# Changing the walk of a column-phase add in a four-direction scan kernel

## The chip, the cores and the metric

The kernel runs on one core of one Trainium2 chip. The metric is the device time of one execution in microseconds (us); the time of a kernel is the median of its runs. The engines are named as in the profile: PE is TensorE (matmuls; PEld is its weight load), DVE is VectorE, ACT is ScalarE, POOL is GpSimd, and SP issues transfers. SBUF is the on-chip buffer of 128 partitions, PSUM the buffer that matmuls write into.

## The reference

The input x has 4 batches, 128 channels and 96 x 96 pixels, in fp32. It is normalized in groups of 4 channels, and then goes through the same gated scan four times: along the rows forwards and backwards, and along the columns forwards and backwards.

```python
seq_all = concat([rows, rows reversed, columns, columns reversed])
t = grouped1x1(seq, in_proj_w, in_proj_b, 4);  u, gate = t[:, :256], t[:, 256:]
u = depthwise_conv(silu(u), dw_w, 5 taps)
s = ssm_in_w u;  a = 0.999 + 0.0009 * sigmoid(ssm_delta_w u + b);  a = clip(a, 0.0001, 0.9999)
bb = tanh(ssm_b_w u + b);  cc = tanh(ssm_c_w u + b)
prefix = cumsum(log(a));  h = exp(prefix) * cumsum(bb * s * exp(-prefix))
u = u + ssm_out_w (cc * h + ssm_d * s)
y = out_proj_w (grouped1x1(u * sigmoid(gate), mix_w, mix_b, 4)) + out_proj_b
out = x + fuse_w concat(y of the four directions, each put back in pixel order) + fuse_b
```

The sum over the four directions is what the changed instruction takes part in.

## The kernel before

The channels lie on the partitions, and the 96 x 96 pixels of one batch along the free dimension. Three large buffers stay in SBUF: `xn` (the normalized input), `sil` (its silu projection) and `acc`, the accumulator of the output, stored row by row as [128, 96 rows, 96 columns]. `acc` starts as x.

For each batch there are two phases. V walks the columns; the host supplies x with its two spatial axes swapped (`xv`), so `xn` and `sil` lie in column order in that phase. H walks the rows. A phase has two passes, one per direction: V goes forwards in pass 0 and backwards in pass 1, H the other way round. A pass goes through 20 chunks of whole lines, 18 of five lines (480 pixels) and 2 of three (288 pixels, the last two in pixel order). With 4 batches these are 16 passes and 320 chunks, 160 of them in V.

The order of the work is the order in which the program is written: each engine executes its instructions in that order, and the tile framework adds the waits. One turn of the main loop (L386 and on) does the following.

- `conv_and_gate` of the chunk: five conv taps for channels 0 to 127 as matmuls with diagonal weights (L249), five taps for channels 128 to 255 as one ScalarE scaling (L260) and four DVE multiply-adds (L262), and the gate (matmul L271, sigmoid L275).
- `ssm_out` of the chunk before: two matmuls (L325, L329) and three DVE operations (L330 to L332).
- In pass 1, `front` of a chunk of the next phase: its normalization (L213), projection (L225) and silu (L229, L232), after a load of its x into `xn`.
- In pass 0 of V, the statistics of the next batch (L134), except for the last batch.
- `scan` of the chunk: projections (L288), three activations (L293, L295, L299), two GpSimd operations on the decay (L301, L302), the product b * s (L303), the recurrence (L309), whose state goes on to the next chunk, and c * h + d * s (L318, L319).
- `accumulate` of the chunk before: two matmuls with the fused output weights into the PSUM tile `py` (L340), and the add into `acc`. In V it is L345; in H it is L351 in pass 0 and L354 in pass 1, which also adds the bias and writes `res`, from where the result goes to memory.

`py` has a single PSUM buffer, so the next chunk's output matmuls wait until the add has read it. In V the chunk is in column order: `py` holds column after column of 96 pixels each, without a gap. The add reads and writes `acc` through the view `accT`, with its two axes swapped, so that it walks the same columns:

```python
accT = acc.rearrange("p h w -> p w h")
part = accT[:, bass.ds(STARTS[c], LINES[c]), :]
nc.vector.tensor_add(part, py[:, :n].rearrange("p (w h) -> p w h", h=HH), part)
```

A column's neighbouring pixels lie 96 words apart in `acc`. In H all operands of the add are contiguous.

Of the kernel before, what the change touches and what calls it, by code (L numbers as in the profile page):

```python
"""x + fuse(four-direction gated SSM scan of groupnorm(x)), one core, fp32 throughout.

For each batch there are two phases, one per pixel order: V walks the columns (its input is
x with the two spatial axes swapped, laid out so by the host) and H walks the rows. In a
phase silu(in_proj(groupnorm(x))) lies whole in SBUF, and both directions of that order read
it, one pass each. A pass goes through chunks of whole lines in scan order and carries the
state h from chunk to chunk:

    u   = depthwise conv of silu       (channels 0..127 on TensorE, 128..255 on ScalarE/VectorE)
    s, b, c, a = projections of u  # L10
    h   = a * h + b * s                (the recurrence behind exp(P) * cumsum(b*s*exp(-P)))
    v   = (u + ssm_out (c*h + d*s)) * sigmoid(gate)
    acc += W v                         (W = fuse_dir . out_proj . mix, multiplied out on chip)

A reverse direction uses flipped taps and scans its chunk backwards, so it stays in the pixel
order of its phase. acc starts as x (the residual). While the second pass of a phase runs, the
next phase's input is loaded into the chunks that are done with, and its silu computed.
"""
# [1 line left out]

# [10 lines left out]
P = 128  # L31
B, DIM, HH, WW = 4, 128, 96, 96
# [6 lines left out]
LINES = [5] * 18 + [3] * 2  # L39
STARTS = [sum(LINES[:i]) for i in range(len(LINES))]  # L40
# [5 lines left out]
def conv_preact_kernel(  # L46
# [27 lines left out]
    xn = big.tile([P, L], F32, name="xn")  # L74
    acc = big.tile([P, HH, WW], F32, name="acc")
    sil = big.tile([P, 2, L + 2 * PAD], F32, name="sil")
    accf = acc.rearrange("p h w -> p (h w)")
    accT = acc.rearrange("p h w -> p w h")

    srcs = {"V": xv, "H": xh}  # L80
    # (pixel order, [(reverse, index of the direction in fuse_w) of both passes])
    kinds = [("V", [(False, 2), (True, 3)]), ("H", [(True, 1), (False, 0)])]
    phases = [(b, order, passes) for b in range(B) for order, passes in kinds]

    def span(c):
        return bass.ds(STARTS[c] * WW, LINES[c] * WW)

# [1 line left out]
    gmean = wp.tile([P, P], F32, name="gmean")  # L89
    per = DIM // GN_GROUPS  # L90
    nc.gpsimd.memset(gmean, 1.0 / per)
    for base, step, mult in ((0, -per, 1), (per - 1, per, -1)):
        nc.gpsimd.affine_select(
            out=gmean,
# [38 lines left out]
        nc.sync.dma_start(t[:, :n], xh[b, :, span(c)])  # L133
        nc.vector.bn_stats(stats_of(b)[:, c, :], t[:, :n])  # L134

# [1 line left out]
    b0, order0, _ = phases[0]  # L137
    for c in range(NCH):
        nc.sync.dma_start(xn[:, span(c)], srcs[order0][b0, :, span(c)])
# [64 lines left out]
            )  # L204
        nc.vector.tensor_add(b_fin, pb[:, 0:1], b_fuse)

# [1 line left out]
    def front(ph, c):  # L208
        """groupnorm and silu(in_proj) of one chunk of phase ph, whose x lies in xn."""
        b = phases[ph][0]  # L210
        n = LINES[c] * WW
        norm = stats[b]
        nc.vector.tensor_scalar(  # L213
            xn[:, span(c)],
            xn[:, span(c)],
            norm[:, 0:1],
            norm[:, 1:2],
            ALU.subtract,
            ALU.mult,
        )  # L220
        pts = []
        for j in range(2):
            q = slice(32 * j, 32 * j + 32)
            pt = ps.tile([P, 512], F32, tag="ps_x", bufs=2, name=f"pu_{ph}_{c}_{j}")
            nc.tensor.matmul(pt[:, :n], w_in[q, :], xn[q, span(c)], start=True, stop=True)  # L225
            pts.append(pt)
        for j in range(2):
            sg = wk.tile([P, CW], F32, tag="sg", name=f"sg_{ph}_{c}_{j}")
            nc.scalar.activation(  # L229
                sg[:, :n], pts[j][:, :n], AF.Sigmoid, bias=b_in[:, j : j + 1]  # L230
            )
            nc.vector.scalar_tensor_tensor(  # L232
                sil[:, j, bass.ds(PAD + STARTS[c] * WW, n)],
                pts[j][:, :n],
                b_in[:, j : j + 1],
                sg[:, :n],
                ALU.add,
                ALU.mult,
            )
# [94 lines left out]
    def accumulate(st):  # L334
        c, d, gv = st["c"], st["dir"], st["gv"]
        n, id_ = LINES[c] * WW, st["id"]
        b, order, _ = phases[st["ph"]]
        py = ps.tile([P, 512], F32, tag="ps_y", name=f"py_{id_}")
        for j in range(2):
            nc.tensor.matmul(  # L340
                py[:, :n], w_fin[:, d, j, :], gv[:, j, :n], start=(j == 0), stop=(j == 1)
            )
        if order == "V":
            part = accT[:, bass.ds(STARTS[c], LINES[c]), :]
            nc.vector.tensor_add(  # L345
                part, py[:, :n].rearrange("p (w h) -> p w h", h=HH), part
            )
            return
        part = accf[:, span(c)]
        if st["pass"] == 0:  # L350
            nc.vector.tensor_add(part, py[:, :n], part)  # L351
            return
        res = wk.tile([P, CW], F32, tag="res", name=f"res_{id_}")
        nc.vector.scalar_tensor_tensor(  # L354
            res[:, :n], py[:, :n], b_fin, part, ALU.add, ALU.add
        )
        nc.sync.dma_start(out[b, :, span(c)], res[:, :n])
        if b + 1 < B:
            nc.sync.dma_start(part, xh[b + 1, :, span(c)])

# [1 line left out]
    steps = []  # L362
    for ph, (b, order, passes) in enumerate(phases):
        for ip, (rev, d) in enumerate(passes):
# [16 lines left out]
    for c in range(NCH):  # L381
        front(0, c)
# [3 lines left out]
    for n, st in enumerate(steps):  # L386
        b, order, _ = phases[st["ph"]]
        conv_and_gate(st)
        if st["pass"] == 1 and st["ph"] + 1 < len(phases):
            nb, norder, _ = phases[st["ph"] + 1]  # L390
            nc.sync.dma_start(xn[:, span(st["c"])], srcs[norder][nb, :, span(st["c"])])
            todo.append((n + 2, st["ph"] + 1, st["c"]))
        if prev is not None:
            ssm_out(prev)
        while todo and todo[0][0] <= n:
            _, ph, c = todo.pop(0)
            front(ph, c)
        if order == "V" and st["pass"] == 0 and b + 1 < B:
            stats_chunk(b + 1, st["c"])
            if st["i"] == NCH - 1:  # L400
                stats_finish(b + 1)
        scan(st)
        if prev is not None:
            accumulate(prev)
        prev = st
    ssm_out(prev)
    accumulate(prev)


# [54 lines left out]
```

## Time and profile before

| what | value |
| --- | --- |
| time, two runs | 3685.1 and 3701.43 us |
| median | 3693.26 us |
| the profiled execution: span from its first to its last instruction | 3681.5 us |
| mean granted TensorE clock in it | 0.938 |
| adds of the V phases, L345 | 160 instructions, 163.9 us busy |
| adds of the H phases, L351 and L354 | 160 instructions, 105.1 us busy |
| loads and stores | 25 GB/s on average over the span |

The profile gives a span for the profiled execution and no separate time; the lowest of the two runs is 3.6 us above that span and the median 11.8 us. The page has the busy time of each engine, the groups of instructions by line (count, busy time, mean duration of one, and the idle time of the engine just before them with what ended it), and the chain of work that ended last, followed back from the last instruction. A stretch of the span can be asked for alone; its row has the length of the stretch, the busy time of each engine with its number of instructions, the granted TensorE clock (1.00 is full speed), the share of the DMA engines and the GB/s that they moved.

### The profile page before, as it was taken

The page shows a single profiled execution, that of the slowest core. Times are in us where ns is not written, and L with a number is a line of the kernel's source. Part 1 is how long each engine was busy: PE and PEld are TensorE (multiplying, and loading weights), DVE is VectorE, ACT ScalarE, POOL GpSimd, SP SyncE. Part 2 cuts the span into 40 slices and gives each one's busy share as a digit, 9 for nine tenths or more (in the row PEclk, how much of TensorE's full clock was granted, in tenths as well). Part 3 has the DMA queues.
Part 4 walks back from the last instruction along what each step waited for, and adds up shares of the span by engine and source line. Part 5 has one row for each costly group of instructions (what it writes and reads, how often), then busy time and mean ns, then how long its engine had stood idle before and what let it go on. Part 6 is the DMA issues. An engine that isn't in the chain of part 4 may idle for free.

```text
span 3681.5 us, 27637 instructions
## 1 busy us (share of the span) xinstructions
PE 3543.3 (96%) x9032; PEld 1550.5 (42%) x9032; DVE 2937.6 (80%) x4442; ACT 1572.0 (43%) x2572; POOL 393.2 (11%) x653
## 2 busy tenths in 40 slices
PE   7999999999999999999999999999999999999999
PEld 3334444444443444444443444444444344444444
DVE  7788887788877888778887788777887778877777
ACT  3334444444443444444443444444444444444443
POOL 0011111111111111111111011111111111111111
PEclk8899999999999999999999999999999999999999
DMA  4210000002100000001210000000121000000000
GB/s 145 82 37 12 19 22 0 0 30 65 59 3 0 17 19 17 0 0 46 65 45 0 0 20 22 11 0 3 59 62 32 0 4 21 22 6 0 3 24 25
DMA packets 56625, 92.14 MB, mean 25 GB/s; under 512 B 7296, under 2 KB 56352, under 8 KB 56480
## 3 DMA queue, kind: packets, MB, share of 16 engines
q1 hardware_dynamic: 54720, 89.68, 8.0%
q8 instruction: 70, 1.15, 0.1%
q10 hardware_dynamic: 1760, 0.70, 0.1%
q14 instruction: 75, 0.61, 0.1%
HBM read 71.48 MB, written 18.87 MB: 25 GB/s over the span
## 4 chain that ended last, share of the span: by engine, by line
DVE 46%; PE 41%; issue 6%; ACT 4%; DMA 2%; POOL 0%; ACTq 0%; DVEq 0%; POOLq 0%
DVE u L262 12%; PE pp L288 8%; PE pc L325 8%; PE pc L249 8%; DVE h L309 8%; PE py L340 6%; PE pz L329 6%; DVE z L319 5%; DVE tb L303 4%; DVE z L318 4%; DVE gv L332 3%; PE pu L225 3%; DVE u L331 3%; DVE sil L232 3%; ACT u L260 2%
## 5 line engine op out<-in xcount | busy, mean ns | idle before, releaser
L249 PE MATMUL pc<-sil,diag 128*128 128x480 f32 (+1 forms) x3200 | 1299.5, 552 | 0.0
L262 DVE SCALAR_TENSOR_TENSOR u<-sil,w_dw,u 128x480 f32<-128x480 f32 (+1 forms) x1280 | 889.0, 695 | 135.4 <-ACT u L260 124.0
L249 PEld LDWEIGHTS pc<-sil,diag 128*128 128x128 f32 x3200 | 610.7, 191 | 643.3 <-issue 624.7
L288 PE MATMUL pp<-u,w_proj 128*128 128x480 f32 (+1 forms) x1280 | 705.2, 680 | 3.1 <-DVE u L262 2.0
L265 ACT COPY u<-pc 128x480 f32<-128x480 f32 (+1 forms) x320 | 173.8, 543 | 1074.9 <-PE pc L249 1074.8
L340 PE MATMUL py<-gv,w_fin 128*128 128x480 f32 (+1 forms) x1280 | 614.2, 605 | 0.9
L301 POOL TENSOR_SCALAR a<-a 32x480 f32<-32x480 f32 (+1 forms) x320 | 189.8, 593 | 3252.3 <-ACT a L295 3252.3
L330 DVE TENSOR_TENSOR gv<-pc,gv 128x480 f32<-128x480 f32 (+1 forms) x320 | 203.8, 637 | 343.5 <-PE pc L325 337.1
L275 ACT ACTIVATE gv<-pg,b_in 128x480 f32<-128x480 f32 (+1 forms) x640 | 379.2, 642 | 143.8 <-PE pg L271 133.4
L325 PE MATMUL pc<-z,w_so 32*128 32x480 f32 (+1 forms) x640 | 332.6, 599 | 101.8 <-DVE z L319 100.5
L340 PEld LDWEIGHTS py<-gv,w_fin 128*128 128x128 f32 x1280 | 282.6, 222 | 331.4 <-issue 234.6
L288 PEld LDWEIGHTS pp<-u,w_proj 128*128 128x128 f32 x1280 | 244.3, 212 | 390.2 <-issue 273.8
L260 ACT ACTIVATE u<-sil,w_dw 128x480 f32<-128x480 f32 (+1 forms) x320 | 216.8, 678 | 404.7 <-DVE gv L332 398.0
L309 DVE TENSOR_TENSOR_SCAN h<-a,h,tb 32x480 f32<-32x480 f32 (+1 forms) x304 | 354.7, 1167 | 1.1
L271 PE MATMUL pg<-xn,w_in 32*128 32x480 f32 (+1 forms) x1280 | 345.5, 600 | 0.6 <-ACT gv L275 0.6
L229 ACT ACTIVATE sg<-pu,b_in 128x480 f32<-128x480 f32 (+1 forms) x320 | 201.7, 638 | 274.8 <-PE pu L225 274.7
L329 PE MATMUL pz<-z,w_so 32*128 32x480 f32 (+1 forms) x640 | 301.1, 550 | 0.0
L225 PE MATMUL pu<-xn,w_in 32*128 32x480 f32 (+1 forms) x640 | 264.2, 632 | 9.1 <-DVE sil L232 7.7
L293 ACT ACTIVATE tb<-pp,b_proj 32x480 f32<-32x480 f32 (+1 forms) x320 | 204.0, 637 | 150.8 <-PE pp L288 145.1
L303 DVE TENSOR_TENSOR tb<-pp,tb 32x480 f32<-32x480 f32 (+1 forms) x320 | 198.9, 621 | 70.3 <-ACT z L299 67.3
L232 DVE SCALAR_TENSOR_TENSOR sil<-pu,b_in,sg 128x480 f32<-128x480 f32 (+1 forms) x320 | 219.0, 691 | 24.9 <-ACT sg L229 23.5
L331 DVE TENSOR_TENSOR u<-pz,u 128x480 f32<-128x480 f32 (+1 forms) x320 | 203.9, 637 | 43.7 <-PE pz L329 2.6
(54 smaller groups left out, 2122.3 us busy)
## 6 DMA issues: line engine op xcount, KB each, us to landing
xn<-in_xv SPq DMA_DIRECT2D x72, 240.0 KB, 2.6
acc<-in_xh SPq DMA_DIRECT2D x72, 240.0 KB, 2.8
xn<-in_xh SPq DMA_DIRECT2D x72, 240.0 KB, 2.6
out<-res SPq DMA_DIRECT2D x72, 240.0 KB, 2.0
xs<-in_xh SPq DMA_DIRECT2D x54, 240.0 KB, 2.6
xn<-in_xv SPq DMA_DIRECT2D x8, 144.0 KB, 2.4
acc<-in_xh SPq DMA_DIRECT2D x8, 144.0 KB, 2.4
xn<-in_xh SPq DMA_DIRECT2D x8, 144.0 KB, 2.1
```

The costliest lines, as they stand in the source:

```text
L225: nc.tensor.matmul(pt[:, :n], w_in[q, :], xn[q, span(c)], start=True, stop=True)
L232: nc.vector.scalar_tensor_tensor(sil[:, j, bass.ds(PAD + STARTS[c] * WW, n)], pts[j][:, :n], b_in[:, j : j + 1], sg[:, :n], ALU.add, ALU.mult,
L249: nc.tensor.matmul(pu[:, :n], diag[:, w, :], sil[:, 0, bass.ds(o + k, n)], start=(k == 0), stop=(k == K - 1),)
L262: nc.vector.scalar_tensor_tensor(u[:, 1, :n], src, coef, u[:, 1, :n], ALU.mult, ALU.add)
L271: nc.tensor.matmul(pg[:, :n], w_in[q, :], xn[q, span(c)], start=True, stop=True)
L275: nc.scalar.activation(gv[:, j, :n], pgs[j][:, :n], AF.Sigmoid, bias=b_in[:, 2 + j : 3 + j])
L288: nc.tensor.matmul(pp[:, :n], w_proj[:, j, :], u[:, j, :n], start=(j == 1), stop=(j == 0))
L303: nc.vector.tensor_mul(tb[:, :n], s, tb[:, :n])
L309: nc.vector.tensor_tensor_scan(dirn(h), dirn(a), dirn(tb), 0.0 if st["first"] else carry[0], ALU.mult, ALU.add,)
L325: nc.tensor.matmul(pu[:, :n], w_so[:, 0:P], z[:, :n], start=False, stop=True, skip_group_check=True)
L329: nc.tensor.matmul(pz[:, :n], w_so[:, P:HID], z[:, :n], start=True, stop=True)
L340: nc.tensor.matmul(py[:, :n], w_fin[:, d, j, :], gv[:, j, :n], start=(j == 0), stop=(j == 1))
```

## The change

The add of the V phases walks the same pixels in another order. It now goes through `acc` row by row: for each of the 96 rows, the five (or three) pixels that belong to the chunk's columns, which lie next to each other, and then 96 words on to the next row. The operand in PSUM is read to match: its step is 96 words from pixel to pixel. The view `accT` is gone. The comments and docstrings that the diff also empties are left out here.

```diff
-    accT = acc.rearrange("p h w -> p w h")
...
         if order == "V":
-            part = accT[:, bass.ds(STARTS[c], LINES[c]), :]
+            part = acc[:, :, bass.ds(STARTS[c], LINES[c])]
             nc.vector.tensor_add(
-                part, py[:, :n].rearrange("p (w h) -> p w h", h=HH), part
+                part, py[:, :n].rearrange("p (w h) -> p h w", h=HH), part
             )
             return
```

The number of instructions, their order on every engine and their waits stay the same. The shape of the instruction's operands goes from 128 x 5 x 96 to 128 x 96 x 5, and for the short chunks from 128 x 3 x 96 to 128 x 96 x 3.

## The prediction

> **What bounds the kernel now.** I read the page's engine totals first, then the DVE groups with shapes kept apart, then the chain of waits and the engine totals in matched stretches of the column and the row phases.
>
> ```profile
> span 3681.5 us, 27637 instructions
> PE 3543.3 (96%) x9032; PEld 1550.5 (42%) x9032; DVE 2937.6 (80%) x4442; ACT 1572.0 (43%) x2572; POOL 393.2 (11%) x653
> ```
>
> By shares TensorE (PE) is full, and VectorE (DVE), on which the edited add runs, has a fifth of the span free. If that were all, a shorter add would be worth nothing. The groups give the size of what is at stake:
>
> ```profile
> L345 DVE TENSOR_TENSOR acc<-py,acc 128x480 f32<-128x480 f32 x144 | 152.7, 1061 | 37.3 <-PE py L340 37.3
> L345 DVE TENSOR_TENSOR acc<-py,acc 128x288 f32<-128x288 f32 x16 | 11.2, 700 | 7.2 <-PE py L340 7.2
> ...
> L351 DVE TENSOR_TENSOR acc<-py,acc 128x480 f32<-128x480 f32 x72 | 46.9, 651 | 15.9 <-PE py L340 15.9
> ...
> L351 DVE TENSOR_TENSOR acc<-py,acc 128x288 f32<-128x288 f32 x8 | 3.5, 442 | 0.0
> ...
> L354 DVE SCALAR_TENSOR_TENSOR res<-py,b_fin,acc 128x480 f32<-128x480 f32 x72 | 50.6, 703 | 6.7 <-PE py L340 6.5
> ...
> L332 DVE TENSOR_TENSOR gv<-u,gv 128x480 f32<-128x480 f32 x288 | 189.1, 657 | 10.0 <-ACT gv L275 0.5
> ...
> L331 DVE TENSOR_TENSOR u<-pz,u 128x480 f32<-128x480 f32 x288 | 189.3, 657 | 42.0 <-PE pz L329 1.5
> ```
>
> L345 is the add of the column phases (V), L351 the same add of the first row pass (H), with every operand contiguous. For the same 480 elements the first takes 1061 ns and the second 651 ns, so stepping through acc costs 410 ns; for 288 elements 700 - 442 = 258 ns. Both adds read py from PSUM without a step. L331, with a PSUM operand, and L332, with SBUF operands alone, both take 657 ns: PSUM as such has no price.
>
> Is the add on the path that sets the end? The chain of waits over one chunk of the first V pass of the last batch:
>
> ```profile
> 2847.65 0.58 DVE z L318
> ...
> 2848.26 0.72 DVE z L319
> ...
> 2849.02 1.07 PE pc L325 x2
> 2850.09 0.82 PE pz L329 x2
> ...
> 2850.93 0.67 DVE u L331
> ...
> 2851.62 0.67 DVE gv L332
> ...
> 2852.37 0.70 ACT u L260
> ...
> 2853.10 0.73 DVE u L262
> ...
> 2853.86 0.72 DVE u L262
> 2854.57 1.01 DVE acc L345
> 2855.59 0.56 DVE tb L303
> ...
> 2856.70 1.20 DVE h L309
> ```
>
> The reader is to see a ring: scan, z, two matmuls of ssm_out, the three gate operations, one ScalarE step, two taps of the next chunk, the add, and again the scan of the next chunk. The add's whole 1.01 us stands in it, and the scan is queued behind it on DVE. So the add sets the pace there though DVE has free time elsewhere in the ring.
>
> What a shorter add is worth can be read off, since the H passes run the same ring with a 651 ns (pass 0) or 703 ns (pass 1) add. I cut stretches of exactly 12 chunks, from the start of one scan to that of the twelfth after it, in the middle of passes. V pass 0 of batch 1, H pass 0 of batches 1 and 2, V pass 0 of batch 3:
>
> ```profile
> core 0: us, PE busy (x) PEld busy (x) DVE busy (x) ACT busy (x) POOL busy (x), PEclk, DMA share, GB/s
> 1044.87:1180.97 136.10, 130.60 (x314) 53.91 (x313) 103.41 (x145) 53.20 (x84) 13.92 (x24) 0.95 0.00 0
> 1495.29:1624.20 128.91, 127.12 (x313) 52.76 (x313) 99.14 (x146) 53.19 (x84) 13.92 (x24) 0.97 0.00 1
> ...
> 2396.57:2525.49 128.92, 127.14 (x313) 52.72 (x313) 99.15 (x146) 53.18 (x84) 13.93 (x24) 0.97 0.00 0
> ...
> 2845.84:2980.45 134.61, 129.15 (x314) 53.50 (x313) 103.38 (x146) 53.18 (x84) 13.92 (x24) 0.96 0.00 1
> ```
>
> Rows 1 and 4 are V, rows 2 and 3 are H. V takes 135.4 us on average, H 128.9: 6.4 us for 12 chunks, 0.54 us a chunk, where the add differs by 0.41 us. The rest fits the granted clock, 0.95 to 0.96 in V against 0.97 in H: PE idles longer in V (5.5 of 136.1 us against 1.8 of 128.9), and the clock falls more often. The same for the second passes (V rows first and third, H rows second and fourth; columns as above):
>
> ```profile
> 358.90:510.13 151.23, 146.31 (x358) 62.19 (x357) 125.04 (x181) 66.63 (x108) 16.30 (x24) 0.90 0.07 20
> 816.15:959.24 143.09, 141.49 (x361) 61.60 (x360) 120.08 (x182) 66.74 (x108) 15.81 (x24) 0.93 0.21 62
> 1256.69:1406.47 149.78, 145.40 (x360) 62.40 (x359) 124.45 (x182) 66.66 (x108) 15.93 (x24) 0.91 0.07 20
> 1711.18:1857.56 146.38, 144.22 (x358) 62.18 (x357) 120.21 (x182) 66.60 (x108) 16.12 (x24) 0.91 0.20 61
> ```
>
> (151.23 + 149.78) / 2 = 150.5 against (143.09 + 146.38) / 2 = 144.7: 0.48 us a chunk where the adds differ by 1061 - 703 = 358 ns. Each nanosecond off the add was worth 0.54/0.41 = 1.3 and 0.48/0.358 = 1.35 ns of time in these stretches.
>
> Whole phases give less. Scan to scan, from the first of a phase to the first of the next:
>
> ```profile
> 1012.70:1466.90 454.20, 437.89 (x1123) 192.77 (x1122) 364.98 (x543) 196.15 (x323) 49.05 (x80) 0.93 0.04 11
> 1466.90:1911.30 444.40, 436.78 (x1127) 190.48 (x1127) 357.14 (x543) 196.17 (x320) 50.25 (x80) 0.95 0.11 32
> ```
>
> V is 9.8 us longer than H, where the adds differ by 18 x (0.410 + 0.358) for the long chunks and about 0.9 for the short ones, 14.7 us in all: a worth of 0.7. But these cuts favour V: the scan that opens an H phase is that of a three-line chunk and its work falls before the cut, so V holds five short chunks and H three. That makes V look up to some 5 us shorter, and corrected the worth is near 1. I take **1.2** between 0.7 and 1.35.
>
> **The change, part by part.** Nothing is added, removed or moved: the same 160 adds stand at the same places on DVE, with the same waits, on the same pixels. Only the walk within the instruction differs. No DMA, no matmul and no wait is touched; whoever waited for the add waits for it as before.
>
> *Stepping through acc, removed.* Now every element of the read and of the written acc lies 96 words from the one before. That is the 410 ns, or 410 / 480 = 0.854 ns an element for both operands together. Afterwards five elements follow each other, then comes a hop to the next row. If only the fifth element pays, 96 x 0.854 = 82 ns remain; the bounds are 0 (runs of five are as good as contiguous) and 410 (they help nothing). No row has short runs. I take 82, since four of five steps become those of L351. For three-line chunks one element in three pays: 96 x 258 / 288 = 86 ns.
>
> *Stepping through PSUM, added.* py is now read 96 words apart. No row of this trace has a stepped PSUM operand. The bounds from the nearest rows: nothing (whatever L345 pays today it pays on acc, py being contiguous in it), and the price that stepping both acc operands has now, 410 ns; less than nothing is excluded, since 651 ns is what the wholly contiguous add takes. I take nothing, from L331 against L332, where PSUM is no dearer than SBUF; this is the weakest step of the forecast, and both ends are kept.
>
> So the long add goes from 1061 to 651 + 82 = 733 ns, 328 ns less, and the short one from 700 to 442 + 86 = 528, 172 ns less. 144 x 0.328 + 16 x 0.172 = 47.2 + 2.8 = 50.0 us of DVE time; by the worth of 1.2 this is **60 us**. Against the profiled execution: 3681.5 - 60 = 3621.5 us of span. The two runs shown are 3685.1 and 3701.4, their median 3693.3, 11.8 above that span; the forecast in the metric is 3693.3 - 60 = **3633 us**, 1.6% less. With 651 ns and a worth of 1.35 it would be 63.1 x 1.35 = 85 us and 3608; with 733 ns and 0.7, 35 us and 3658. That is the forecast's own range.
>
> What is next when the add is short: in the H rows PE is busy 127.1 of 128.9 us, 1.8 us of slack in 12 chunks, 0.15 us a chunk, so there DVE's ring and PE arrive nearly together. An add below 651 ns would buy little more; the gain is used up about where the forecast ends.
>
> **The rivals.** *A step on PSUM is priced like a step on acc.* The 410 ns belong to two operands and can't be split by these rows: one operand alone may cost half, 205, or all of it. The add then takes 651 + 82 + 205 = 938 to 651 + 82 + 410 = 1143 ns. The long ones change by -123 to +82 ns and the short ones by about as much in proportion: -18.5 to +13 us of DVE, by 1.2 -22 to +16, so **3671 to 3709 us**. For it: the price seems to come with the hop of every element, which the change moves to another operand and does not remove. Against it: one operand hops instead of two, and it lies in another memory.
>
> The Trainium skill speaks for this rival (DVE Microarchitecture Reference, "5.2 Measured stream behaviour on trn2"): full rate needs runs of at least two adjacent words starting on an 8-byte boundary, and a single source hopping at every element went from 1.054 to 1.73 ns a column, there measured on SBUF. By that the added step costs an estimated 324 ns and the add about as much as now; the same page has all hops between aligned pairs free. The trace agrees that single-element hops on acc are dear (0.854 ns), and no row shows PSUM.
>
> *PE or ScalarE takes up the gain in the second V passes.* There the chain also goes through PE and ScalarE:
>
> ```profile
> 1262.54 3.51 PE pp L288 x4
> ...
> 1266.08 0.65 ACT tb L293
> ...
> 1266.76 0.66 ACT a L295
> ...
> 1267.44 0.67 ACT z L299
> ...
> 1268.13 0.65 DVE tb L303
> ```
>
> At this place the projection and three activations end last, and the add is hidden. If that holds throughout, the 80 adds of these passes give nothing, and half of the 60 us is left: **3663 us**. Against it stands the 0.48 us a chunk between the second passes, though their direction and their DMA traffic (share 0.07 against 0.20) differ as well.
>
> *A stepped PSUM read is dearer than anything here.* Priced at twice the step on acc, 820 ns, the add takes 651 + 82 + 820 = 1553 ns. It sits in front of tb and the scan, and the ring grows by all of it: 144 x 0.492 + 16 x 0.344 = 76 us, by 1.2 92, so **3785 us**, slower than before. It turns slower from an add of 1061 ns, a PSUM step of (1061 - 733) / 480 = 0.68 ns an element. For it: nothing in the trace limits that price. Against it: the price that is known, 0.854 ns, is for two operands.
>
> **How the numbers follow.** Forecast 0.52, PSUM priced like acc 0.24, second passes hidden 0.12, PSUM dearer than acc 0.12. The range goes from 3606, the forecast's best end, to 3705, which takes in the hidden second passes and nearly all of the like-priced PSUM step; outside are most of the dear step and a little at each end, under 2 in 10. A measurement of this kernel can tell about 2% from no change: 3619 and 3767 us. Below 3619 lies the part of the forecast with an add under some 690 ns or a worth above 1.3: 0.20. Above 3767 an add over about 1450 ns is needed: 0.05. The rest, 0.75, is within.
>
> **What would show it.** Right: the group of the V add has 144 instructions of some 730 ns (650 to 800), the 12-chunk stretches of V pass 0 take about 130 us and those of V pass 1 about 146, and the granted clock in them rises to that of the H stretches. The PSUM step is wrong if the add stays near 1000 ns or above; the runs of five are free if it is within 20 ns of 651. The worth is wrong if the add falls as said and V chunks don't shorten by 0.3 to 0.45 us. The forecast falls altogether if V chunks get longer, or if a H stretch changes, in which nothing was edited.

## The result and the profile after

The changed kernel takes 3605.8 us (median of 2 runs, 3603.8 to 3607.8) against 3693.3 us before: the ratio is 0.9764, with a 95% interval of 0.9736 to 0.9791. That is 87.5 us less, where 60 were forecast, and 0.2 us under the lower end of the range.

The profiled execution has a span of 3602.0 us, 79.5 us under the 3681.5 us of before. The DVE groups of the changed kernel (L344 is the V add, before L345; L350 and L353 are the untouched H adds):

```profile
L344 DVE TENSOR_TENSOR acc<-py,acc 128x480 f32<-128x480 f32 x144 | 93.0, 646 | 20.8 <-PE py L339 20.8
...
L353 DVE SCALAR_TENSOR_TENSOR res<-py,b_fin,acc 128x480 f32<-128x480 f32 x72 | 50.6, 703 | 6.6 <-PE py L339 6.4
L350 DVE TENSOR_TENSOR acc<-py,acc 128x480 f32<-128x480 f32 x72 | 46.9, 652 | 15.9 <-PE py L339 15.9
...
L344 DVE TENSOR_TENSOR acc<-py,acc 128x288 f32<-128x288 f32 x16 | 7.6, 477 | 7.4 <-PE py L339 7.4
```

The long V add went from 1061 to 646 ns and is as short as the contiguous one; the short one went from 700 to 477, somewhat above the 443 of a contiguous short add (L350). Together they took 163.9 us and now take 100.6: 63.3 us less DVE time.

Stretches of 12 chunks again, cut from scan to scan as in the prediction. Columns: stretch, its length, busy time of PE, PEld, DVE, ACT and POOL, granted clock, DMA share, GB/s. The rows are V pass 0 (two), V pass 1 (two), H pass 0 and H pass 1:

```profile
1020.61:1149.52 128.91, 127.12 (x313) 52.76 (x313) 99.15 (x145) 53.19 (x84) 13.90 (x24) 0.97 0.00 1
1900.48:2027.93 127.45, 125.49 (x313) 52.12 (x313) 99.15 (x146) 53.20 (x84) 13.89 (x24) 0.99 0.00 0
1222.06:1365.62 143.56, 142.06 (x361) 62.21 (x360) 119.01 (x181) 66.67 (x108) 16.18 (x24) 0.93 0.08 21
2101.99:2245.39 143.40, 142.04 (x361) 61.71 (x360) 119.93 (x181) 66.67 (x108) 16.20 (x24) 0.93 0.08 21
1453.32:1580.76 127.44, 125.65 (x314) 52.25 (x313) 99.14 (x145) 53.18 (x84) 13.89 (x24) 0.99 0.00 1
1669.09:1814.90 145.81, 143.44 (x360) 62.02 (x359) 120.21 (x181) 66.64 (x108) 16.38 (x24) 0.92 0.20 61
```

V pass 0 went from 135.4 to 128.2 us and V pass 1 from 150.5 to 143.5, about 0.6 us a chunk in both, for 0.415 us off the add. V pass 0 now looks like H pass 0 in every column. The granted clock rose from 0.95 and 0.96 to 0.97 and 0.99, and in the second passes from 0.90 and 0.91 to 0.93. PE's idle time in V pass 0 fell from 5.5 to 1.8 us. H pass 0 differs by 1.5 us from before, and so does its clock (127.4 us at 0.99 here, 128.9 at 0.97 there); H pass 1 lies between its two rows of before. So the gain comes from V.

The chain over one chunk of V pass 0 is the same ring, with a shorter add:

```profile
1027.14 0.70 ACT u L259
...
1027.87 0.73 DVE u L261
...
1028.62 0.72 DVE u L261
1029.34 0.57 DVE acc L344
...
1029.91 0.65 DVE tb L302
```

The add's 1.01 us in it has become 0.57.

### The profile page after: what moved, and what is told of

The parts are those of the page before. It is cut to its first block, busy times and chain, and to the rows that moved or that the text cites. A ratio compares the mean times of both kernels' runs of the same rounds, so it can differ in the third digit from the quotient of the medians.

```text
span 3602.0 us, 27637 instructions
## 1 busy us (share of the span) xinstructions
PE 3501.1 (97%) x9032; PEld 1539.4 (43%) x9032; DVE 2877.5 (80%) x4442; ACT 1572.0 (44%) x2572; POOL 393.0 (11%) x653
## 4 chain that ended last, share of the span: by engine, by line
PE 44%; DVE 44%; issue 6%; ACT 4%; DMA 2%; ACTq 0%; POOL 0%; DVEq 0%; POOLq 0%
DVE u L261 12%; PE pc L248 11%; PE pc L324 8%; PE pp L287 8%; DVE h L308 7%; PE pz L328 6%; PE py L339 5%; DVE z L318 4%; DVE tb L302 4%; DVE z L317 4%; DVE gv L331 3%; DVE u L330 3%; PE pu L224 3%; PE pg L270 3%; ACT u L259 3%
## 5 line engine op out<-in xcount | busy, mean ns | idle before, releaser
L339 PE MATMUL py<-gv,w_fin 128*128 128x480 f32 (+1 forms) x1280 | 588.9, 584 | 1.0
L339 PEld LDWEIGHTS py<-gv,w_fin 128*128 128x128 f32 x1280 | 270.6, 213 | 311.5 <-issue 226.7
L224 PE MATMUL pu<-xn,w_in 32*128 32x480 f32 (+1 forms) x640 | 251.0, 625 | 10.2 <-DVE sil L231 7.9
```

The source lines that it names most:

```text
L339: nc.tensor.matmul(py[:, :n], w_fin[:, d, j, :], gv[:, j, :n], start=(j == 0), stop=(j == 1))
```

## The experiments

The theory after the result: each element of `acc` that was reached alone cost time, the PSUM step costs none, and the gain followed because the add stood in the ring of both passes. The rivals: PSUM has a price that something hides; runs of five pay something; the second passes hide their add; DVE's total work counts, and not the place; the stepped access slowed other engines too. Where a run's time is compared with the kernel before, both ran on the same chip.

### The PSUM step alone

```diff
-            part = acc[:, :, bass.ds(STARTS[c], LINES[c])]
+            part = accf[:, span(c)].rearrange("p (h w) -> p h w", h=HH)
```

> The V adds read PSUM 96 words apart, as in the changed kernel, while acc is read and written contiguously (the sums land on other pixels of acc, so the output is another one). Theory A, a step on the PSUM operand costs nothing: the long add takes 640 to 655 ns and the short one about 443 ns, so the 477 ns of the changed kernel's short add come from its runs of three in acc. Theory B, the PSUM step has a price of its own and the short add pays it: the short one stays near 477 ns. Time of the kernel by both within 1% of the changed kernel's 3606 us.

The kernel took 3609.6 us. Its V adds:

```profile
L344 DVE TENSOR_TENSOR acc<-py,acc 128x480 f32<-128x480 f32 x144 | 92.7, 643 | 22.6 <-PE py L339 22.6
...
L344 DVE TENSOR_TENSOR acc<-py,acc 128x288 f32<-128x288 f32 x16 | 7.2, 452 | 6.8 <-PE py L339 6.8
```

A PSUM operand stepped by 96 words costs nothing at 480 elements: 643 ns. The short add falls to 452, so 25 of the 34 ns that the changed kernel's short add has over 443 come from the runs of three in `acc`. They come from the one of the two short chunks that starts at column 90. In the changed kernel's V pass 0 of batch 2, the add of the chunk that starts at column 90 stands first, that of the chunk at column 93 second:

```profile
2063.08 0.52 DVE L344 TENSOR_TENSOR acc<-py,acc 128x288 f32<-128x288 f32 x1 [0.45 <-PE py L339]
2073.85 0.46 DVE L344 TENSOR_TENSOR acc<-py,acc 128x288 f32<-128x288 f32 x1 [1.02 <-PE py L339]
```

Over all eight V passes the first takes 482 to 516 ns and the second 449 to 459. If `acc` is divided into groups of four words from its start, the three words from column 90 leave the last one alone in the next group, and the three from column 93 lie in one group. The runs of other lengths, below, come to the same rule.

### The two operands in acc, one at a time

A stepped read alone, with the sum written to a contiguous scratch tile:

```diff
+            res = wk.tile([P, CW], F32, tag="res", name=f"res_{id_}")
+            flat = res[:, :n].rearrange("p (w h) -> p w h", h=HH)
...
-                part, py[:, :n].rearrange("p (w h) -> p w h", h=HH), part
+                flat, py[:, :n].rearrange("p (w h) -> p w h", h=HH), part
```

> The V adds read acc down its columns as before, read PSUM contiguously and write into a contiguous scratch tile instead of acc (the V sums are left out of the output). Theory A, each stepped operand pays its own part of the 410 ns and the parts add up: this and the run with a stepped write give together about 410 ns above 651, most likely some 205 each (an add of 850 ns). Theory B, one price for a hop in any operand, not added up: both stay near 1060 ns. Theory C, the write alone pays: this one is at 651 ns and the other at 1060.

A stepped write alone, with the contiguous gate tile as the other input:

```diff
+            flat = gv[:, 0, :n].rearrange("p (w h) -> p w h", h=HH)
...
-                part, py[:, :n].rearrange("p (w h) -> p w h", h=HH), part
+                part, py[:, :n].rearrange("p (w h) -> p w h", h=HH), flat
```

> The V adds write acc down its columns as before, but their SBUF input is the contiguous gate tile instead of acc, and PSUM is read contiguously (acc is overwritten instead of added to, so the output is another one). Theory A: the parts of read and write add up to about 410 ns, this one near 850 ns. Theory B: near 1060 ns in both. Theory C: near 1060 ns here and 651 in the run with a stepped read.

The V add with the stepped read, then that with the stepped write:

```profile
L347 DVE TENSOR_TENSOR res<-py,acc 128x480 f32<-128x480 f32 x144 | 140.0, 972 | 36.3 <-PE py L340 35.6
```

```profile
L346 DVE TENSOR_TENSOR acc<-py,gv 128x480 f32<-128x480 f32 x144 | 141.7, 984 | 32.0 <-PE py L340 31.8
```

None of the three theories is right. Either operand alone costs 972 - 651 = 321 or 984 - 651 = 333 ns, and both together 410 and not 654: so most of the second price is not paid on top of the first. The times were 3678.8 and 3661.6 us in one run each against 3699.9 for the kernel before. The first fits its 89 ns off the add (13 us of DVE time, by 1.3 some 17); the second is some 20 us lower than its 77 ns explain (12 us of DVE time), which stays open.

### Runs of other lengths and starts

```diff
-            part = acc[:, :, bass.ds(STARTS[c], LINES[c])]
+            r, o = RUNS[2 * b + st["pass"]]
+            rows = accf.rearrange("p (k m) -> p k m", m=16 * r)
+            part = rows[:, : n // r, o : o + r]
...
-                part, py[:, :n].rearrange("p (w h) -> p h w", h=HH), part
+                part, py[:, :n].rearrange("p (k r) -> p k r", r=r), part
```

In what follows (r, o) stands for runs of r words that start at word o; the second kernel differs in its list of (r, o) and in the step, which is 96 words for r = 5.

> The V adds go through acc in runs of r words with a step of 16 r words between the runs, starting at word o, and read PSUM contiguously; the eight V passes take (r, o) = (1, 0), (2, 0), (2, 1), (3, 0), (3, 1), (4, 0), (4, 1), (6, 0) in this order (other pixels of acc are summed, so the output is another one). Theory A, an element pays only if no neighbour in its aligned pair of words is used: r = 1 near 1060 ns; r = 2, 4 and 6 from word 0 at 651; r = 3 about 700; r = 2 from word 1 clearly above r = 2 from word 0. Theory B, any run of two or more is free: 651 ns for all but r = 1. Theory C, the price is one per hop, 0.854 ns: 856 ns for r = 2, 788 for r = 3, 753 for r = 4, 719 for r = 6, and the start does not matter.

> As the first kernel with short runs in acc (step of 16 r words, 96 for r = 5; PSUM contiguous; three-line chunks take r = 6 where r does not divide them), with (r, o) = (2, 3), (3, 2), (3, 3), (4, 2), (4, 3), (5, 0), (5, 3), (6, 3) over the eight V passes. There r = 4 from word 1 alone took 706 ns instead of 651. Theory A, what costs is a run that crosses from one group of four aligned words into the next and leaves a single word there: (2, 3), (3, 2), (3, 3) and (4, 3) above 690 ns, (4, 2) at 651. Theory B, any crossing costs: also (4, 2), (5, 0), (5, 3) and (6, 3) above 690. Theory C, it is peculiar to runs of four: only (4, 3) and perhaps (4, 2) above 690.

The adds of one V pass each, with the minimum, median and maximum duration in ns; the long chunks set median and maximum. From the first kernel (1, 0), (2, 1) and (4, 1):

```profile
L347 DVE TENSOR_TENSOR acc<-py,acc x20: 651/986/1048, 117.5 to 329.4; 128x480 f32<-128x480 f32 x18, 128x288 f32<-128x288 f32 x2
...
L347 DVE TENSOR_TENSOR acc<-py,acc x20: 459/651/659, 1014.2 to 1210.0; 128x480 f32<-128x480 f32 x18, 128x288 f32<-128x288 f32 x2
...
L347 DVE TENSOR_TENSOR acc<-py,acc x20: 492/706/718, 2771.6 to 2963.5; 128x480 f32<-128x480 f32 x18, 128x288 f32<-128x288 f32 x2
```

From the second, in order, (2, 3), (3, 2), (3, 3), (4, 2), (4, 3), (5, 0), (5, 3) and (6, 3):

```profile
L349 DVE TENSOR_TENSOR acc<-py,acc x20: 668/1014/1051, 115.7 to 327.9; 128x480 f32<-128x480 f32 x18, 128x288 f32<-128x288 f32 x2
L349 DVE TENSOR_TENSOR acc<-py,acc x20: 502/694/765, 333.2 to 560.8; 128x480 f32<-128x480 f32 x18, 128x288 f32<-128x288 f32 x2
L349 DVE TENSOR_TENSOR acc<-py,acc x20: 486/743/805, 1016.1 to 1212.4; 128x480 f32<-128x480 f32 x18, 128x288 f32<-128x288 f32 x2
L349 DVE TENSOR_TENSOR acc<-py,acc x20: 450/635/659, 1217.8 to 1441.1; 128x480 f32<-128x480 f32 x18, 128x288 f32<-128x288 f32 x2
L349 DVE TENSOR_TENSOR acc<-py,acc x20: 491/712/719, 1898.8 to 2093.3; 128x480 f32<-128x480 f32 x18, 128x288 f32<-128x288 f32 x2
L349 DVE TENSOR_TENSOR acc<-py,acc x20: 450/640/668, 2098.6 to 2321.8; 128x480 f32<-128x480 f32 x18, 128x288 f32<-128x288 f32 x2
L349 DVE TENSOR_TENSOR acc<-py,acc x20: 485/651/664, 2777.3 to 2969.1; 128x480 f32<-128x480 f32 x18, 128x288 f32<-128x288 f32 x2
L349 DVE TENSOR_TENSOR acc<-py,acc x20: 477/674/729, 2976.4 to 3202.4; 128x480 f32<-128x480 f32 x18, 128x288 f32<-128x288 f32 x2
```

The passes left out of the first kernel, (2, 0), (3, 0), (3, 1), (4, 0) and (6, 0), have medians of 635 to 651 ns; the second passes of V have 635 where the first have 651, whatever the walk. Theory A of the first kernel (aligned pairs) falls: three words from word 0 leave the third alone in its pair and are free, and two words from word 1 are free too. Its Theory B (any two words are free) falls by (4, 1), and Theory C (one price per hop) by all the free ones. Of the second kernel's theories, B (any crossing costs) falls by (4, 2), (5, 0) and (5, 3), and C (runs of four alone) by (3, 2) and (3, 3). Theory A fits the passes other than those of r = 5 as a rule, if not each number: what costs is a single word left in a group of four, counted from the start of `acc`. Two words that lie in two groups, (2, 3), cost as much as single words, 1014 ns; runs split into one and some others, (3, 2), (3, 3), (4, 1), (4, 3) and (6, 3), cost 39 to 92 ns above the 635 or 651 of their pass; runs split two and two, (4, 2), are free. Runs of five that leave one word alone, (5, 0) and (5, 3), should pay by that rule and hardly do (640 and 651). Why is open. It is the case of the changed kernel, whose long chunks start at every place of a group: in each kind of V pass, those that leave one word alone take 1 to 9 ns more on average than the others. Each (r, o) was run in one pass of one execution.

### The new walk in the first pass alone

```diff
...
+            if st["pass"] == 0:
+                part = acc[:, :, bass.ds(STARTS[c], LINES[c])]
+                nc.vector.tensor_add(
+                    part, py[:, :n].rearrange("p (w h) -> p h w", h=HH), part
+                )
+            else:
                 part = accT[:, bass.ds(STARTS[c], LINES[c]), :]
...
```

> The new walk in the first pass of each V phase alone, the old one in the second. Theory A, the add sits in the ring of both passes and each is worth about 1.3 of its DVE time: the four first passes give 11.7 + 10.9 + 9.7 + 10.8 = 43 us, so 3693 - 43 = 3650 us. Theory B, the second passes hide their add behind the projections and activations: nearly all of the 87 us is gained here, about 3610 us.

3655.4 us against 3693.7, a ratio of 0.9898 (0.9883 to 0.9913): 38 us from the first passes, so some 50 of the 87.5 us come from the second. Theory A holds and the rival of the hidden second passes falls. In the changed kernel the second passes show why (DVE at the place where a chunk's scan starts):

```profile
1281.35 0.65 DVE L302 TENSOR_TENSOR tb<-pp,tb 32x480 f32<-32x480 f32 x1 [1.26 <-ACT z L298]
1281.92 0.65 DVE L344 TENSOR_TENSOR acc<-py,acc 128x480 f32<-128x480 f32 x1
1282.48 1.20 DVE L308 TENSOR_TENSOR_SCAN h<-a,h,tb 32x480 f32<-32x480 f32 x1
```

PE and the activations do end last, as that rival had it, but the add stands behind tb and in front of the scan, in the kernel before as well, so the scan still waits for it. The prediction's reading of this rival's lines, that the add is hidden there, was wrong.

### A DVE instruction more, at the add and in the gap

```diff
             part = acc[:, :, bass.ds(STARTS[c], LINES[c])]
+            pad = wk.tile([P, CW // 2], F32, tag="pad", bufs=1, name=f"pad_{id_}")
+            nc.vector.tensor_add(pad[:, : n // 2], py[:, : n // 2], gv[:, 0, : n // 2])
```

> The changed kernel with one more contiguous DVE add of half a chunk (240 elements, about 400 ns by the fixed part and slope of the rows) into a scratch tile ahead of each V add. Theory A, only the length of DVE's work at this place counts: the time goes back to that of the kernel before, 3675 to 3700 us, and the V chunks to 11.2 and 12.5 us. Theory B, the stepped add did more than take time (it slowed other engines' access to SBUF): the time stays clearly below, under 3665 us.

```diff
+        if phases[st["ph"]][1] == "V":
+            pad = wk.tile([MH, CW // 2], F32, tag="pad", bufs=1, name=f"pad_{id_}")
+            nc.vector.tensor_mul(pad[:, : n // 2], z[:, : n // 2], z[:, : n // 2])
         pz = ps.tile([P, 512], F32, tag="ps_z", name=f"pz_{id_}")
```

> The changed kernel with one more contiguous DVE product of half a chunk (about 400 ns) in the V passes, placed behind the last z operation, where DVE waits for ssm_out's matmuls (1.16 us a chunk). Theory A, the ring sets the pace and DVE's wait there is free: within 0.4% of the changed kernel, 3600 to 3620 us. Theory B, DVE's total work counts wherever it stands: about 3675 us or more.

The pad at the add took 394 ns and the kernel 3663.9 us (ratio 0.9922, 0.9899 to 0.9945), 58 us above the changed one where some 80 were expected. In the first passes 12 chunks of V pass 0 take 136.2 us, as before the change, which is what Theory A says; but DVE's order changed there too (the add stands behind tb instead of ahead of it, and one conv tap has moved in front of the second z operation). The second passes don't test it at all:

```profile
1307.72 0.39 DVE L345 TENSOR_TENSOR pad<-py,gv 128x240 f32<-128x240 f32 x1
1308.04 1.20 DVE L308 TENSOR_TENSOR_SCAN h<-a,h,tb 32x480 f32<-32x480 f32 x1
1309.16 0.62 DVE L346 TENSOR_TENSOR acc<-py,acc 128x480 f32<-128x480 f32 x1
```

Here the pad stands ahead of the scan and the add behind it, so less than before the change delays the scan. As a test of Theory B the run is undecided. It also sets right what was said of the kernel before: the engines don't always execute in the order in which the program is written. `accumulate` is written behind `scan`, yet in the traces of both kernels DVE executes its add ahead of the recurrence. Between the kernel before and the changed one DVE's order is the same throughout; where an instruction or an ordering edge was added, others changed places too. The pad in the gap is clear: 396 ns of DVE work in each V chunk and 3605.0 us (ratio 0.9762, 0.9745 to 0.9778), the time of the changed kernel. In the 12-chunk stretches of all passes but the first, DVE's other instructions stand as in the changed kernel. So 0.4 us of work in that wait of 1.16 us is free, and the rival that DVE's total work counts falls.

### The add moved into the gap

DVE is made to issue the V add behind the last z operation of the next chunk, by an ordering edge and no wait. There DVE stands idle in the kernel before:

```profile
2848.26 0.70 DVE L319 SCALAR_TENSOR_TENSOR z<-pp,d_sb,z 32x480 f32<-32x480 f32 x1
2850.12 0.66 DVE L330 TENSOR_TENSOR gv<-pc,gv 128x480 f32<-128x480 f32 x1 [1.16 <-PE pc L325]
```

The edit:

```diff
-            nc.vector.tensor_add(
+            add = nc.vector.tensor_add(
...
+            behind_z(add)
```

With the old walk:

> The kernel before, with its old walk and its add of 1061 ns, but in the V passes DVE is made to issue the add behind the last z operation of the next chunk, where it waits 1.16 us a chunk for ssm_out's matmuls. Theory A, the price of the old walk was the place of the add in the ring, and the gap hides it: the V chunks fall to those of the changed kernel or a little below (10.4 to 10.7 us and 11.7 to 12.0), 3575 to 3615 us with the add still at about 1060 ns. Theory B, the add's DVE time or its stepped access counts wherever it stands: 3670 us or more.

With the new walk, in V alone and then in both phases:

> The same move of the add in the V passes, with the new walk. Theory A: within 0.5% of the kernel with the old walk at that place, since both adds fit into the wait of 1.16 us; a little under the changed kernel, 3575 to 3605 us. Theory B: about 80 us faster than the old walk at that place.

> The new walk, with the add moved into DVE's wait in the H passes too. Theory A, the ring gets 0.65 us shorter there and PE sets the pace next (0.15 us of idle time a chunk in the H stretches): 0.1 to 0.2 us a chunk more, 3550 to 3595 us. Theory B, PE already sets the pace in H: the same as the run with the V adds alone.

| kernel | median us | ratio to before (95%) |
| --- | --- | --- |
| old walk, V adds in the gap | 3569.3 | 0.9652 (0.9630 to 0.9674) |
| new walk, V adds in the gap | 3562.6 | 0.9639 (0.9614 to 0.9665) |
| new walk, V and H adds in the gap | 3560.9 | 0.9631 (0.9608 to 0.9653) |

DVE in the gap kernel with the old walk:

```profile
1077.17 0.71 DVE L329 SCALAR_TENSOR_TENSOR z<-pp,d_sb,z 32x480 f32<-32x480 f32 x1
1077.80 1.07 DVE L357 TENSOR_TENSOR acc<-py,acc 128x480 f32<-128x480 f32 x1
1079.03 0.66 DVE L342 TENSOR_TENSOR gv<-pc,gv 128x480 f32<-128x480 f32 x1 [0.16 <-PE pc L337]
```

The old add still takes 1.07 us, all of it in a wait that shrank from 1.16 to 0.16 us, and this kernel is 36 us faster than the changed one (41 by the two ratios to before), in which the 646 ns add still stands in the ring. One conv tap changed places as well: it went from between the scan and z to the place that the add left. In the 12-chunk stretches DVE's order is the same in both V-only kernels of the table, so their difference is the walk alone: with the add out of the ring it is worth 7 us, 0.2%, with overlapping intervals. This is the strongest evidence that the old walk cost time by its length at its place; what it may cost other engines is no more than these few us. All three times are below or at the low end of the ranges given.

In the kernel with both phases moved, V pass 0, H pass 0, V pass 1 and H pass 1:

```profile
1021.47:1146.52 125.05, 124.48 (x314) 51.86 (x313) 103.39 (x146) 53.13 (x84) 17.09 (x24) 0.99 0.00 1
1441.54:1566.60 125.06, 124.48 (x314) 51.83 (x313) 103.38 (x145) 53.14 (x84) 17.08 (x24) 0.99 0.00 1
1220.05:1358.88 138.83, 138.69 (x360) 60.67 (x359) 121.04 (x182) 66.59 (x108) 17.00 (x24) 0.94 0.08 22
1652.33:1802.66 150.33, 145.41 (x362) 61.70 (x361) 122.86 (x182) 66.46 (x108) 17.30 (x24) 0.91 0.19 59
```

PE is the full engine in the first three: 0.6 us or less of 125 to 139 is idle. H pass 0 gained 0.2 us a chunk, as expected, but H pass 1 went from 145.8 to 150.3 us, so the total stands still. The traces show a new wait there. DVE in 12 chunks of H pass 1, with the H adds moved and then with the V adds alone (us in total, times, longest):

```profile
DVE xn L212 <- DMA xn<-in_xv: 13.6, 12, 2.0
...
DVE xn L212 <- DMA xn<-in_xv: 0.8, 2, 0.5
```

In H pass 1 SP issues the store of `res` and, behind it, the load of the next phase's x into `xn`. With the add moved, the store waits for `res` until behind the last z operation, the load is issued behind the store, and DVE's normalization stands idle for it, 1.1 us a chunk. In the last batch, which has no such load, 12 chunks of H pass 1 fell from 129.3 us with the V adds alone to 125.3. No run was made that changes the load alone.

### A small matmul more where PE waits

```diff
+        pz = ps.tile([P, 512], F32, tag="ps_z", name=f"pz_{id_}")
+        if phases[st["ph"]][1] == "V":
+            nc.tensor.matmul(pz[:, :64], diag[:, 0, :], gv[:, 0, :64], start=True, stop=True)
...
-        pz = ps.tile([P, 512], F32, tag="ps_z", name=f"pz_{id_}")
```

> The kernel before with one more small matmul (64 columns, overwritten by the next one) in the V passes where PE waits for z. Theory A, a third of what the change was worth came from the clock, which falls when PE idles: the V chunks of the first pass get a higher granted clock (0.97 or more instead of 0.95 to 0.96) and shorten from 11.25 us to 10.9, those of the second pass likewise, and the kernel is 20 to 40 us faster than before. Theory B, the extra worth is not the clock's: the granted clock in the V stretches stays or the chunks don't shorten, the same time or up to 20 us slower, since PE has more to do.

3719.4 us, a ratio of 1.0072 (1.0056 to 1.0089). V pass 0 and V pass 1 of this kernel:

```profile
1055.11:1191.25 136.14, 134.91 (x338) 57.47 (x337) 103.45 (x146) 53.19 (x84) 13.90 (x24) 0.95 0.00 0
...
1266.86:1421.87 155.01, 152.62 (x385) 66.68 (x384) 124.31 (x182) 66.53 (x108) 16.54 (x24) 0.90 0.07 20
```

PE's idle time in V pass 0 fell from 5.5 to 1.2 us, and the granted clock stayed at 0.95. Theory A falls: less idle time on PE did not by itself bring the clock back. V pass 1 got longer, with 7 us more PE work, but DVE's order changed there too, so it says less.

## Why the prediction was right, and where its sizes were off

**The ring.** Right. The add stands ahead of the scan in both V passes; 0.4 us of work put into the gap is free; the old add moved there costs 7 us against the new one, within the spread.

**The PSUM step at no price.** Right: 643 ns with that step alone. It was called the weakest step, taken without a row that had such a step, so its coming true owes something to luck. The rivals that priced it, at 3671 to 3709 and 3785 us, fell, and with them the estimate of 324 ns for the added step.

**The remainder of 82 ns for the runs of five.** Wrong, and the largest error. It charged every fifth element as a lone one; the long add came to 646 ns and not 733. For the short chunks 86 ns were charged and 34 came, most of it in the chunk at column 90. DVE gained 63.3 us and not 50.0. The lower bound given, 0, was the right end for the long adds.

**The worth of 1.2.** Somewhat low: 79.5 / 63.3 = 1.26 between the two profiled spans, and 87.5 / 63.3 = 1.38 between the medians. The matched stretches had given 1.3 and 1.35. The 0.7 of the whole phases, which pulled the figure down, came from a comparison that favoured V by more than the 5 us allowed for:

```profile
989.60:1423.50 433.90, 425.98 (x1121) 189.81 (x1120) 349.71 (x542) 196.14 (x323) 49.95 (x80) 0.95 0.04 12
1423.50:1868.10 444.60, 437.59 (x1125) 191.22 (x1124) 356.75 (x543) 196.40 (x320) 48.84 (x80) 0.95 0.11 32
```

With adds of nearly one length a V phase (first row) is 10.7 us shorter than an H phase. Part of that is the passes themselves, since 12 chunks of H pass 1 take 2 us more than those of V pass 1 in the stretches above; the rest was not taken apart. V itself fell from 454.2 to 433.9 us: 20.3 us for 36 long adds less 415 ns and 4 short ones less 223, 15.8 us in all, a worth of 1.28. With 646 and 477 ns the sum is 63.3 x 1.2 = 76 us and 3617; with the stretches' 1.35 it is 85 us and 3608. The 8 us by which the medians gained more than the spans are within the spread of the kernel before: in the later runs, where span and time are given together, the time is 1.7 us above the span, so its profiled execution took some 3683 us, and its timed runs went from 3685 to 3707 us, as a rule longer where the granted clock was lower (3687.4 us at 0.937, 3707.0 at 0.933). Both terms of the sum erred to the same side, and together they put the result at the range's lower end.

**Where a worth above 1 comes from.** In the stretches of V pass 0 the chunk shortened by 0.6 us and the add by 0.415, while the granted clock rose from 0.95 and 0.96 to 0.97 and 0.99. The trace shows what these means are made of: the clock is at full rate, and now and then at half rate for 3.4 us (in the second passes also for 6.8). Such a dip and the stretch up to the next, in V pass 0 before and then after:

```profile
1095.20:1098.60 3.40, 3.40 (x6) 1.55 (x5) 2.31 (x4) 1.55 (x3) 0.00 (x0) 0.51 0.00 0
1098.70:1129.30 30.60, 29.23 (x75) 12.03 (x74) 23.61 (x33) 11.64 (x19) 3.48 (x6) 1.00 0.00 1
...
1036.70:1040.10 3.40, 3.40 (x6) 1.42 (x5) 2.25 (x4) 1.68 (x3) 0.00 (x0) 0.50 0.00 0
1040.20:1122.10 81.90, 80.65 (x205) 33.43 (x204) 63.80 (x93) 33.68 (x54) 9.27 (x16) 1.00 0.00 0
```

By the trace's record of the clock the two V pass 0 stretches before hold four and three dips, the two after two and one. What one dip costs can be read off the two after, which do the same work: 128.91 us with two and 127.45 with one, so 1.5 us. Two dips fewer are 3 us by this estimate, and the shorter adds give 12 x 0.415 = 5 us; 8 in all, where 7.2 were measured. So the size of the rest of the worth fits the clock, as the prediction had it. But the link that it gave, that the clock falls because PE idles, is not borne out by the run with one more matmul, which has four dips again at 1.2 us of idle time. In the stretches the dips come at nearly whole numbers of chunks: in V pass 0 mostly 34 us or three chunks apart before, and still so with the matmul added, 85 us or eight chunks apart in the changed kernel, and mostly 24 us or two chunks apart in its V pass 1. That they answer to something in the turn of the ring, and not to the sum of the idle time, would fit this; it was not tested, and what brings the dips on is open.

**PE next.** Half right. The changed V pass 0 has 1.8 us of PE idle time in 128.9, as H has. But the prediction took this as nearly all that a shorter add could still give, and it was not: with the V adds out of the ring the kernel took 3562.6 us, 43 less than the changed one (46 by the ratios). In the stretches shown, of the kernel with the H adds moved too, V pass 0 fell from 128.9 to 125.1 us and V pass 1 from 143.6 to 138.8, and most of that is PE's busy time, 127.1 to 124.5 and 142.1 to 138.7, at a granted clock that rose from 0.97 to 0.99 and from 0.93 to 0.94. The busy time of PE was no fixed floor.

## What to carry to other kernels

Before pricing a slow instruction, find whether it stands in the loop-carried chain; the 1061 ns add cost 88 us more than the 646 ns one in its first place, and 7 us more, within the spread, in a wait of the same engine a few instructions later. Where an fp32 add has one operand in PSUM and others in SBUF, try giving the runs to the SBUF operands and the step to PSUM: a PSUM step of 96 words was free here, and other steps were not run. When an idle share of the busiest engine is read as what is left to gain, look whether its granted clock is at full rate. Compare matched stretches from the middle of a stage, since cuts at its edges carry work of the neighbours along.

## What the runs showed that was not expected

- Adds of 480 elements in runs of five words that leave one alone in its group of four had medians at most 5 ns above the contiguous, while those in runs of three and four that do so cost 55 to 92 ns.
- A stepped read and a stepped write of `acc` cost 321 and 333 ns alone and 410 together.
- The second V passes have adds 16 ns shorter than the first for the same walk (635 against 651 ns); with the adds in the gap the first passes have 635 too, so it goes with the place and not with the pass.
- PE's idle time and the clock dips fell together when the add got shorter, but a matmul that took 4 of 5.5 us of that idle time left the clock at 0.95.
- In H pass 1 the add moved back in DVE's order held up a store, and with it a load that SP issues behind it.
